# Layer 1 of a four-layer network: the product with bt ahead of the step-size means, and the gate's product in four parts

## The chip, the cores and the metric

The kernel runs on one core of a Trainium2 chip. One launch computes all four layers. The metric is the device time of that launch in microseconds (us). Six runs of the kernel before the change took 4355.97 to 4390.86 us, with a median of 4374.4 us.

A core has five engines, each with an instruction queue of its own that is worked off in order: TensorE (PE in the profile; its weight loads are shown apart as PEld), VectorE (DVE), ScalarE (ACT), GpSimd (POOL) and SyncE (SP, which here only starts transfers). Engines wait for each other through semaphores. Matrix products read SBUF, the on-chip memory, and write PSUM, a small set of accumulation buffers that the other engines read.

## The reference

x has 2 sequences of 2048 tokens with 256 features, in float32. Each of the four layers normalizes x and adds an "attention" and an "FFN" part. Only layer 1 is touched by the change. Cut to what matters, it is:

```python
xn = _layernorm(x)
x = x + attn(xn) + ffn(xn)

# attn: a selective scan
h = _layernorm(xn, ln_gamma, ln_beta)
xs, gate = split(h @ W_in)                       # 512 channels each
xs = silu(causal_conv(xs, conv_w) + conv_b)
delta = mean(softplus(xs @ Wd + bd), axis=-1)    # one step size per token
A = -exp(A_log)                                  # 16 states
Bx = (xs @ B_mat.T) * delta                      # the product with bt
h_t = exp(delta_t * A) * h_(t-1) + Bx_t          # scan over the tokens
y = h @ C_mat + D * xs
y = y * silu(gate)                               # the gate's product
attn = xn + y @ W_out

# ffn: per token and head the best of 4096 experts, by product keys
sim = q @ keys                                   # two halves, 128 keys each
index, score = best pair of keys                 # 8 heads
hidden = gelu(xn @ W_in.T + sum_heads(relu(score) * (xn . in_a[index]) * in_b[index]))
ffn = hidden @ W_out.T + sum_heads(relu(score) * (hidden . out_a[index]) * out_b[index])
```

`softplus(z)` is computed as `relu(z) + log(1 + exp(-|z|))`, with a correction for the rounding of `1 + exp(-|z|)`. That is where the four quantities `sp`, `la`, `lb` and `lc` of the kernel come from: the mean step size is the mean of `sp + la - lb + lc` over the 512 channels.

## The kernel before

x stays in SBUF for the whole launch. Layer 1 (`layer1`) cuts the 4096 tokens into 16 blocks of 256. Three generator functions do the work of one block: `scan_block` is the attention part, `choose_block` finds the experts, and `rows_block` fetches their rows and computes the FFN part. One iteration of the loop in `layer1` weaves three of them together (`weave`): the scan of block n, the choice of block n−1 and the rows of block n−2, so that each engine's queue holds work of three blocks in turn. Within that text a scheduler then orders each engine's instructions by when their inputs will be ready, so the final order isn't the text's order word for word. Layers 0, 2 and 3 lie ahead of and behind this loop.

The scan block is a chain, stage by stage:

1. Two normalizations, each followed by transposes on PE: `xn` and `xt`, then `hn` and `hT` (helpers `norm2` and `turn2`).
2. The product with `wi` (16 matmuls of two passes each). Its first half is copied to `xr` (L665), its second goes through Silu to `sgt`, the gate (L667).
3. The convolution of `xr` to `xs`: four ACT instructions (L671) and twelve on DVE (L674); then Silu over all of xs (L678).
4. The product with `wd`. For each of four channel groups m, ACT reads the sum twice from PSUM: Abs to `la` (L690) and Relu to `sp` (L691).
5. Exp of `la` (L693, behind a table load), `lb` on DVE (L695), Ln to `lc` (L697).
6. The means, `p4`: sixteen small matmuls with the constant `inv` (L702) over sp, la, lb and lc. A copy to `s4` (L705), a matmul with `four` that sums the four 32-row strips and spreads the result over 16 rows (`pd`), and the product of xs with `bt` (`pb`, four matmuls of two passes).
7. `dl`, a copy of pd (L712); `dA`, its Exp (L714, behind a table load); `dl` times `pb` on DVE (L715); the scan itself on DVE (L717).
8. For each m a matmul with `ct` and, on DVE, `xs*D + ps` written back to xs (L724).
9. The gate's product: one POOL instruction over all of xs, 128 partitions by 1024 (L727). A second POOL instruction adds xn to x (L728).
10. The product with `wout` (eight matmuls of two passes each) and its addition to x on DVE (L733).

All matmul results of the scan block come from one pool of PSUM tiles, `psc`, with two buffers (`ps_c` in the profile). A third tile is given out once one of the two has been read for the last time. The choice uses `ps_k` and the rows `ps_h`, with three buffers each. Most SBUF tiles of the scan block exist once (xs, sgt, sp, la, lb, lc, s4).

Around the chain, the same engines do the work of the other two blocks. On PE: `ps_k` (the keys), and for the rows a product into `ps_h`, transposes and the products with `dg` (L839). On DVE: max and its index (L778, L782), for each fetched row tile `G` a custom multiply-and-sum with two inputs in SBUF (L815 over 256 features, L834 over 512), its use (L817), and the addition of the rows to x (L842). On POOL: the gathers of `G`, one indirect DMA each (L805), 32 for a block, into 10 buffers. Each gather's issue occupies POOL, and it stands in the same queue as L727 and L728.

In the profile the product with bt is `ps_c<-xs,bt`, with wd `ps_c<-xs,l_wd`, with wout `ps_c<-l_wc,xs`, the means `ps_c<-sp,inv` and so on; all of them are issued from the helper `mm` (L68), the means excepted.

Of the kernel before, what the change touches and what calls it, by code (L numbers as in the profile page):

```python
# [20 lines left out]
ALU = mybir.AluOpType  # L21
# [42 lines left out]
def mm(nc, out, pairs):  # L64

    n = len(pairs)
    for i, (lhsT, rhs) in enumerate(pairs):
        nc.tensor.matmul(out, lhsT, rhs, start=(i == 0), stop=(i == n - 1))  # L68
# [93 lines left out]
def fetch_experts(g, r, pool, t):  # L162

    nc = g.nc
    y = pool.tile([P, 2, D], F32, name="yg", tag="yg", bufs=2)
    for j in range(2):
        nc.gpsimd.indirect_dma_start(y[:, j, :], None, r.yd,
                                     bass.IndirectOffsetOnAxis(ap=r.pos[:, j, t : t + 1], axis=0))
        nc.vector.scalar_tensor_tensor(g.x[:, t, :], y[:, j, :], r.wt[j][:, t : t + 1], g.x[:, t, :],
                                       ALU.mult, ALU.add)  # L170
# [390 lines left out]
def layer1(g, tc, a, r):  # L561
# [5 lines left out]
    with ExitStack() as es:  # L567
# [51 lines left out]
        for n in range(NB + 2):  # L619
            streams = []  # L620
            if n < NB:
                streams.append((1, scan_block(g, L, blocks[n], blocks[n - 1] if n % (NB // B) else None)))
            if 0 <= n - 1 < NB:
                streams.append((1, choose_block(g, L, blocks[n - 1])))
            if 0 <= n - 2:
                streams.append((2, rows_block(g, a, L, blocks[n - 2])))
            weave(*streams)


def scan_block(g, L, k, prev):  # L630
    nc, wk, TB, nt, pp = g.nc, L.wk, L.TB, L.nt, g.pp

    def pcol(name, i=0):
        return pp[:, PP[name] + i : PP[name] + i + 1]

    ti = k.tok // P
    for t in range(ti + nt if k.n else 0, min(ti + 2 * nt, NT)):
        fetch_experts(g, L.r, wk, t)
    xb = g.x[:, ti : ti + nt, :]
    k.xn = xn = wk.tile([P, nt, D], F32, name="xn1", tag="xn1", bufs=3)  # L640
    norm2(g, wk, xb, xn, nt)
    k.xt = wk.tile([P, 2, TB], F32, name="xt1", tag="xt1", bufs=3)
    turn2(g, L.psc, xn, k.xt, nt)
    yield

    hn = wk.tile([P, nt, D], F32, name="hn", tag="hn")
    norm2(g, wk, xn, hn, nt)
    hT = wk.tile([P, 2, TB], F32, name="hT", tag="hT")
    turn2(g, L.psc, hn, hT, nt, pp[:, PP["gamma"] : PP["gamma"] + 2], pp[:, PP["beta"] : PP["beta"] + 2])
    yield  # L650
    k.xr = xr = wk.tile([P, 4, TB + 3], F32, name="xr", tag="xr", bufs=2)
    if prev is None:
        nc.gpsimd.memset(xr[:, :, 0:3], 0.0)
    else:
        nc.gpsimd.tensor_copy(xr[:, :, 0:3], prev.xr[:, :, TB : TB + 3])
    sgt = wk.tile([P, 4, TB], F32, name="sgt", tag="sgt")
    for m2 in range(4):
        ps = L.psc()
        for i in range(2):
            m = 2 * m2 + i  # L660
            mm(nc, ps[:, i * TB : (i + 1) * TB],
               [(L.wi[:, c, m * P : (m + 1) * P], hT[:, c, :]) for c in range(2)])
        ps2 = ps.rearrange("p (i n) -> p i n", i=2)
        if m2 < 2:
            nc.scalar.copy(xr[:, 2 * m2 : 2 * m2 + 2, 3:], ps2)  # L665
        else:
            nc.scalar.activation(sgt[:, 2 * m2 - 4 : 2 * m2 - 2, :], ps2, AF.Silu)  # L667
    yield
    xs = wk.tile([P, 4, TB], F32, name="xs", tag="xs")
    for m in range(4):  # L670
        nc.scalar.activation(xs[:, m, :], xr[:, m, 0:TB], AF.Identity, bias=pcol("conv_b", m),  # L671
                             scale=pcol("conv_w", 4 * m))
        for c in range(1, 4):
            nc.vector.scalar_tensor_tensor(xs[:, m, :], xr[:, m, c : c + TB], pcol("conv_w", 4 * m + c),  # L674
                                           xs[:, m, :], ALU.mult, ALU.add)
        if m == 1:
            yield
    nc.scalar.activation(xs, xs, AF.Silu)  # L678
    yield


    sp = wk.tile([P, 4, TB], F32, name="sp", tag="sp")
    la = wk.tile([P, 4, TB], F32, name="la1", tag="la1")
    for m2 in range(2):
        ps = L.psc()
        for i in range(2):
            m = 2 * m2 + i
            z = ps[:, i * TB : (i + 1) * TB]
            mm(nc, z, [(L.wd[:, c, m * P : (m + 1) * P], xs[:, c, :]) for c in range(4)])
            nc.scalar.activation(la[:, m, :], z, AF.Abs, bias=pcol("bd", m))  # L690
            nc.scalar.activation(sp[:, m, :], z, AF.Relu, bias=pcol("bd", m))  # L691
    yield
    nc.scalar.activation(la, la, AF.Exp, scale=-1.0)  # L693
    lb = wk.tile([P, 4, TB], F32, name="lb", tag="lb")
    nc.vector.tensor_scalar(lb, la, 1.0, 1.0, ALU.add, ALU.subtract)  # L695
    lc = wk.tile([P, 4, TB], F32, name="lc", tag="lc")
    nc.scalar.activation(lc, la, AF.Ln, bias=g.one)  # L697

    p4 = L.psc()
    for q, (t, w) in enumerate(((sp, 0), (la, 0), (lb, 1), (lc, 0))):  # L700
        for m in range(4):
            nc.tensor.matmul(p4[32 * m : 32 * m + 32, 0:TB], L.inv[:, w, :], t[:, m, :],  # L702
                             start=(q == 0), stop=(q == 3))
    s4 = wk.tile([P, TB], F32, name="s4", tag="s4")
    nc.scalar.copy(s4, p4[:, 0:TB])  # L705
    pd = L.psc()
    mm(nc, pd[0:16, 0:TB], [(L.four, s4)])
    pb = L.psc()
    mm(nc, pb[0:16, 0:TB], [(L.bt[:, m, :], xs[:, m, :]) for m in range(4)])
    yield  # L710
    dl = wk.tile([16, TB], F32, name="dl", tag="dl")
    nc.scalar.copy(dl, pd[0:16, 0:TB])  # L712
    dA = wk.tile([16, TB], F32, name="dA", tag="dA")
    nc.scalar.activation(dA, pd[0:16, 0:TB], AF.Exp, scale=L.na)  # L714
    nc.vector.tensor_tensor(dl, dl, pb[0:16, 0:TB], ALU.mult)  # L715
    k.hs = hs = wk.tile([16, TB], F32, name="hs", tag="hs", bufs=2)
    nc.vector.tensor_tensor_scan(hs, dA, dl, 0.0 if prev is None else prev.hs[:, TB - 1 : TB],  # L717
                                 ALU.mult, ALU.add)
    for m2 in range(2):
        ps = L.psc()  # L720
        for i in range(2):
            m = 2 * m2 + i
            mm(nc, ps[:, i * TB : (i + 1) * TB], [(L.ct[:, m * P : (m + 1) * P], hs)])
            nc.vector.scalar_tensor_tensor(xs[:, m, :], xs[:, m, :], pcol("D", m),  # L724
                                           ps[:, i * TB : (i + 1) * TB], ALU.mult, ALU.add)
    yield
    nc.gpsimd.tensor_tensor(xs, xs, sgt, ALU.mult)  # L727
    nc.gpsimd.tensor_tensor(xb, xb, xn, ALU.add)  # L728
    ps = L.psc()
    for i in range(nt):  # L730
        mm(nc, ps[:, i * D : (i + 1) * D], [(xs[:, m, i * P : (i + 1) * P], L.wout[:, m, :]) for m in range(4)])
    xf = xb.rearrange("p i d -> p (i d)")
    nc.vector.tensor_tensor(xf, xf, ps, ALU.add)  # L733
    yield


def norm2(g, pool, src, dst, nt):

    nc = g.nc
    st = pool.tile([P, nt, 6], F32, name="ln_st", tag="ln_st")  # L740
    mv = pool.tile([P, nt, 2], F32, name="ln_mv", tag="ln_mv")
    for i in range(nt):
        nc.vector.bn_stats(st[:, i, :], src[:, i, :])
        nc.vector.bn_aggr(mv[:, i, :], st[:, i, :])
    rs = pool.tile([P, nt], F32, name="ln_rs", tag="ln_rs")
    nc.scalar.activation(rs, mv[:, :, 1], AF.Sqrt, bias=g.eps)
    nc.vector.reciprocal(rs, rs)
    mr = pool.tile([P, nt], F32, name="ln_mr", tag="ln_mr")
    nc.vector.scalar_tensor_tensor(mr, mv[:, :, 0], -1.0, rs, ALU.mult, ALU.mult)
    for i in range(nt):  # L750
        nc.scalar.activation(dst[:, i, :], src[:, i, :], AF.Identity, bias=mr[:, i : i + 1],
                             scale=rs[:, i : i + 1])


def turn2(g, psum, src, dst, nt, scale=None, bias=None):

    nc = g.nc
    for c in range(2):
        ps = psum()
        for i in range(nt):  # L760
            nc.tensor.transpose(ps[:, i * P : (i + 1) * P], src[:, i, c * P : (c + 1) * P], g.ident)
        if scale is not None:
            nc.scalar.activation(dst[:, c, :], ps[:, : nt * P], AF.Identity, bias=bias[:, c : c + 1],
                                 scale=scale[:, c : c + 1])
        else:
            nc.scalar.copy(dst[:, c, :], ps[:, : nt * P])
# [942 lines left out]
```

## Time and profile before

| what | value |
|---|---|
| median of six runs | 4374.4 us (4355.97 to 4390.86) |
| profiled execution | 4369.64 us |
| its span | 4367.9 us |
| granted TensorE clock, mean | 0.937 |
| L727 (gate's product), 16 times | 2346 to 2457 ns, from 1265.2 to 2257.5 us |
| L728 (x plus xn), 16 times | 1262 to 1292 ns |
| L715 (dl times pb), 16 times | 390 to 409 ns |
| L724 (xs times D plus ps), 64 times | 449 to 483 ns |
| L805 (a gather's issue on POOL), 432 times in 1300 to 2240 us | 1050 to 1071 ns in the mean |
| PE idle ahead of `ps_c<-xs,l_wd`, 1300 to 2240 us | 25.0 us |
| PE idle ahead of `ps_c<-sp,inv`, 1300 to 2240 us | 25.7 us |
| PE idle ahead of `ps_c<-l_wc,xs`, 1300 to 2240 us | 9.9 us |

How to read the profile: it shows one execution. A group's line gives the line of the kernel, the engine, the operation, what is written and read (`out<-in`), the shapes and the count; then, behind a bar, the busy time and the mean duration of one in ns; then, behind a second bar, how long the engine had been idle just ahead of these instructions, and whose end released it (`<-PE ps_c L68 8.8` means that 8.8 us of the idle time ended with a PE instruction on ps_c from line 68). "issue" is idle time that ended with nothing that the profile names. In a timeline each line has the start, the duration, the engine, the line and the operation, and in brackets the idle time before it. PE's matmuls are pipelined, and their ends are modelled.

Layer 1's loop fills about 1200 to 2300 us of the span.

### The profile page before, as it was taken

What the parts mean: (1) busy time and instruction counts of PE and PEld (TensorE: products, weight loads), DVE (VectorE), ACT (ScalarE), POOL (GpSimd) and SP (SyncE); (2) the same over time, 40 slices, a digit from 0 to 9 for tenths busy, and PEclk for the clock granted to TensorE, in tenths of its full rate; (3) what the DMA queues carried; (4) which work ended last, traced back from release to release, by engine and by line L of the source; (5) the groups of instructions that cost most, each with busy time, mean ns of one, the idle gap of its engine ahead of it and who ended that gap; (6) DMA issues with size and microseconds to landing.
All of it is one profiled execution on the core that took longest, in us unless ns stands there. A gap on an engine that the chain in (4) does not pass through costs nothing.

```text
span 4367.9 us, 58911 instructions
## 1 busy us (share of the span) xinstructions
PE 3900.2 (89%) x21516; PEld 2323.7 (53%) x21516; DVE 2509.2 (57%) x6436; ACT 1976.8 (45%) x3819; POOL 1304.5 (30%) x1306
## 2 busy tenths in 40 slices
PE   6488988999878898889885999999999999999998
PEld 5366666766645555555553777777433333333332
DVE  6354444454468888788796332333866656566560
ACT  3144333443344554445532323232555565566556
POOL 1402222222166655555464111112201111111201
PEclk7677999999999999999997999999999999999999
DMA  4200122222335666565575000000000000000000
GB/s 177 92 32 32 63 79 79 79 79 79 129 117 173 185 194 183 176 201 186 166 217 168 1 1 1 1 1 22 8 7 9 6 4 19 14 6 9 4 2 25
DMA packets 110803, 330.23 MB, mean 76 GB/s; under 512 B 30609, under 2 KB 63010, under 8 KB 104114
## 3 DMA queue, kind: packets, MB, share of 16 engines
q0 software_dynamic: 52720, 264.15, 19.5%
q1 hardware_dynamic: 55330, 59.41, 4.2%
q8 instruction: 170, 2.79, 0.3%
q10 hardware_dynamic: 2464, 2.91, 0.2%
q14 instruction: 119, 0.97, 0.1%
HBM read 286.56 MB, written 33.03 MB: 73 GB/s over the span
## 4 chain that ended last, share of the span: by engine, by line
PE 45%; DVE 4%; issue 2%; POOL 1%; ACT 1%; DMA 1%; another core or an unknown queue 0%; SPq 0%; POOLq 0%; ACTq 0%; DVEq 0%
PE ps_e L1345 12%; PE ps_v L1408 6%; PE ps_a L68 6%; PE ps_f L68 5%; PE ps_m L68 4%; PE ps_m L1350 2%; PE ps_o L1043 1%; PE ps_c L68 1%; PE ps_m L1359 1%; PE ps_k L68 1%; PE ps_s L1345 1%; DVE mp L1376 1%; PE ps_s L1350 1%; PE ps_x L68 0%; POOL G L805 0%
## 5 line engine op out<-in xcount | busy, mean ns | idle before, releaser
L1376 DVE TENSOR_REDUCE mp<-ps_m 128x1 f32<-128x512 f32 (+3 forms) x1120 | 628.4, 606 | 436.2 <-PE ps_e L1345 253.2
L1365 ACT ACTIVATE pt<-ps_e 128x512 f32<-128x512 f32 (+3 forms) x1120 | 537.2, 531 | 426.9 <-PE ps_e L1345 395.4
L1345 PE MATMUL ps_e<-qT,kT 32*128 32x512 f32 (+3 forms) x2240 | 632.2, 581 | 9.0 <-ACT pt L1365 8.8
L1350 PE MATMUL ps_m<-kT,qT 32*128 32x512 f32 (+3 forms) x2240 | 564.3, 579 | 1.1 <-DVE mp L1376 1.1
L1345 PEld LDWEIGHTS ps_e<-qT,kT 32*128 32x128 f32 x2240 | 212.3, 185 | 328.8 <-issue 122.9
L805 POOL DMA_INDIRECT G<-in_tab_in,ind x256 | 271.6, 1061 | 293.4 <-DVE ind L792 121.7
L1408 PE MATMUL ps_v<-pt,vals 128*32 128x512 f32 (+3 forms) x2560 | 307.1, 544 | 1.6 <-POOL pt L1369 0.9
L1369 POOL TENSOR_SCALAR_AFFINE_SELECT pt<-pt 128x256 f32<-128x256 f32 x256 | 104.2, 408 | 664.7 <-ACT pt L1365 664.5
L805 POOL DMA_INDIRECT G<-in_tab_out,ind x256 | 270.8, 1058 | 86.7 <-issue 58.3
L68 PE MATMUL ps_e<-xgT,we 128*128 128x256 f32 x936 | 239.7, 402 | 27.0 <-ACT xgT L306 17.7
L68 PE MATMUL ps_k<-wk,xt 128*128 128x512 f32 x512 | 261.3, 622 | 2.7 <-issue 1.4
L68 PE MATMUL ps_f<-hb,l_b 128*128 128x512 f32 x1024 | 253.2, 399 | 1.5 <-DVE hb L1034 1.5
L1033 ACT ACTIVATE hb<-ps_f 128x512 fp32r<-128x512 f32 x128 | 75.4, 596 | 321.7 <-PE ps_f L68 321.7
L68 PEld LDWEIGHTS ps_f<-hb,l_b 128*128 128x128 f32 x1024 | 190.0, 189 | 47.0 <-issue 6.7
L68 PEld LDWEIGHTS ps_e<-xgT,we 128*128 128x128 f32 x936 | 176.3, 197 | 70.2 <-ACT xgT L306 23.3
L834 DVE CUSTOM_DVE_ANT_0 scr<-hid,G,gate 128x512 f32<-128x512 f32 x256 | 198.4, 775 | 22.6 <-ACT hid L821 8.3
L1034 DVE SCALAR_TENSOR_TENSOR hb<-ps_f,hb 128x512 fp32r<-128x512 f32 x128 | 86.8, 684 | 203.7 <-ACT hb L1033 203.4
L1350 PEld LDWEIGHTS ps_m<-kT,qT 32*128 32x128 f32 x2240 | 182.3, 185 | 26.2 <-issue 22.2
L494 DVE COPY_PREDICATED AT<-lm,ps_g 128x256 f32<-128x256 uint8 x224 | 105.0, 520 | 149.5 <-PE ps_g L489 144.7
L489 PE MATMUL ps_g<-qt,E 64*128 64x64 f32 x1792 | 143.7, 303 | 32.8 <-DVE E L485 23.9
L815 DVE CUSTOM_DVE_ANT_0 scr<-xn,G,gate 128x256 f32<-128x256 f32 x256 | 144.2, 563 | 42.0 <-DMA G<-in_tab_in,ind 35.2
L817 DVE SCALAR_TENSOR_TENSOR hid<-G,lin,hid 128x512 f32<-128x512 f32 x224 | 167.1, 746 | 2.0
(421 smaller groups left out, 7665.2 us busy)
## 6 DMA issues: line engine op xcount, KB each, us to landing
xgd<-zero SPq DMA_DIRECT2D x13, 768.0 KB, 12.0
xg<-xgd SPq DMA_DIRECT2D x39, 256.0 KB, 2.9
yd<-ye SPq DMA_DIRECT2D x39, 256.0 KB, 3.3
G<-in_tab_in,ind POOLq DMA_INDIRECT x256
G<-in_tab_out,ind POOLq DMA_INDIRECT x256
kT<-qk SPq DMA_DIRECT2D x256, 16.0 KB, 1.8
out<-x SPq DMA_DIRECT2D x8, 512.0 KB, 3.0
x<-in_x ACTq DMA_DIRECT2D x4, 512.0 KB, 9.2
```

What stands on the lines that cost most here:

```text
L68: nc.tensor.matmul(out, lhsT, rhs, start=(i == 0), stop=(i == n - 1))
L489: nc.tensor.matmul(two[r][:, n * 64 : (n + 1) * 64], E[r * 64 : (r + 1) * 64, n * P : (n + 1) * P], qt[r * 64 : (r + 1) * 64, n * 64 : (n ...
L494: nc.vector.copy_predicated(AT[:, r].rearrange("p e (n t m) -> p e n t m", t=2, m=m)[:, :, :, 1, :], lm[:, li * 64 : (li + 1) * 64].unsque ...
L805: nc.gpsimd.indirect_dma_start(G, None, a[tab], bass.IndirectOffsetOnAxis(ap=k.ind[:, h, j : j + 1], axis=0))
L815: nc.vector.tensor_tensor_reduce(scr[:, 0:D], k.xn[:, j, :], G[:, 0:D], k.gate[:, h, j : j + 1], 0.0, ALU.mult, ALU.add, lin[:, h : h + 1])
L817: nc.vector.scalar_tensor_tensor(hs, G[:, D:768], lin[:, h : h + 1], hid if h == 0 else hs, ALU.mult, ALU.add)
L834: nc.vector.tensor_tensor_reduce(scr, hs, G[:, 0:512], k.gate[:, h, j : j + 1], 0.0, ALU.mult, ALU.add, lout[:, h : h + 1])
L1345: nc.tensor.matmul(te[i // step][:, i % step, c0:512], ge.kT[row(j), kt * P : (kt + 1) * P], ge.qT[row(j), qb * 512 + c0 : (qb + 1) * 512] ...
L1350: nc.tensor.matmul(tm[i // step][:, i % step, 0:w], gm.qT[row(j), qi * P : (qi + 1) * P], gm.kT[row(j), ch * 512 : ch * 512 + w], start=Tr ...
L1365: nc.scalar.activation(pt[:, o : o + step, c0:512], te[i // step][:, :, c0:512], AF.Exp, scale=0.25)
L1376: nc.vector.tensor_reduce(gm.mp[:, qi, j : j + step, ch], tm[i // step][:, :, 0:w], AX.X, ALU.max, negate=True)
L1408: nc.tensor.matmul(av[row(j), c0:512], vals[:, kt, at + 17 * j : at + 17 * j + 32], pts[j][:, c0:512], start=first, stop=last)
```

## The change

Two edits in `scan_block`. The first moves the allocation of `pb` and its four matmuls from behind the matmul with `four` to a place ahead of the means: behind Ln (L697) in the program's text. The second takes the POOL instruction over all of xs apart into four, one for each m, each placed in the loop right behind the addition L724 of the same m.

```diff
     lc = wk.tile([P, 4, TB], F32, name="lc", tag="lc")
     nc.scalar.activation(lc, la, AF.Ln, bias=g.one)
 
+    pb = L.psc()
+    mm(nc, pb[0:16, 0:TB], [(L.bt[:, m, :], xs[:, m, :]) for m in range(4)])
+
     p4 = L.psc()
     for q, (t, w) in enumerate(((sp, 0), (la, 0), (lb, 1), (lc, 0))):
         for m in range(4):
...
     nc.scalar.copy(s4, p4[:, 0:TB])
     pd = L.psc()
     mm(nc, pd[0:16, 0:TB], [(L.four, s4)])
-    pb = L.psc()
-    mm(nc, pb[0:16, 0:TB], [(L.bt[:, m, :], xs[:, m, :]) for m in range(4)])
     yield
...
             nc.vector.scalar_tensor_tensor(xs[:, m, :], xs[:, m, :], pcol("D", m),
                                            ps[:, i * TB : (i + 1) * TB], ALU.mult, ALU.add)
+            nc.gpsimd.tensor_tensor(xs[:, m, :], xs[:, m, :], sgt[:, m, :], ALU.mult)
     yield
-    nc.gpsimd.tensor_tensor(xs, xs, sgt, ALU.mult)
     nc.gpsimd.tensor_tensor(xb, xb, xn, ALU.add)
```

Line numbers in the text are those of the kernel before. In the changed kernel the four parts of the gate's product are again on line 727, the addition on 725 and x plus xn on 729; the means are on 705, s4 on 708, dl on 713, dA on 715, dl times pb on 716 and the scan on 718.

## The prediction

> **What bounds the kernel now.** I read the page's busy shares first, then the busy time of the engines in four stretches of layer 1 (the only part that the edit touches), then PE's groups of layer 1 with the idle time ahead of them, then the two edited lines, and last the order of time in one block.
>
> ```profile
> PE 3900.2 (89%) x21516; PEld 2323.7 (53%) x21516; DVE 2509.2 (57%) x6436; ACT 1976.8 (45%) x3819; POOL 1304.5 (30%) x1306
> ```
> ```profile
> 1300.00:1360.00 60.00, 48.82 (x204) 30.94 (x202) 48.64 (x152) 27.85 (x50) 35.94 (x34) 0.97 0.51 148
> 1600.00:1660.00 60.00, 54.95 (x223) 33.45 (x223) 55.90 (x187) 31.81 (x56) 38.55 (x35) 1.00 0.73 211
> 1900.00:1960.00 60.00, 51.69 (x213) 33.73 (x212) 53.41 (x176) 30.83 (x55) 35.11 (x33) 0.97 0.61 177
> 2180.00:2240.00 60.00, 52.65 (x206) 33.86 (x205) 52.03 (x164) 27.62 (x53) 36.88 (x34) 0.97 0.68 210
> ```
> The columns are the stretch, its length, busy us of PE, PEld, DVE, ACT and POOL, the granted clock, the DMA share and GB/s. Over the whole span PE looks like the bound; here neither PE nor DVE is full, though both are near 52 of 60 us. A block of 256 tokens takes 66.15 us (the gate's product L727 starts 16 times, from 1265.2 to 2257.5: 992.3/15). At 52/60 PE works some 57 us of that and idles 8 or 9. So the period is set by a serial chain (the scan block, one PSUM tile after another), filled with the work of two other blocks, and whatever shortens the chain can win at most those 9 us.
>
> ```profile
> L68 PE MATMUL ps_c<-xs,l_wd 128*128 128x256 f32 x448 | 116.3, 413 | 25.0 <-issue 19.8 <-ACT xs L678 3.6 <-ACT sp L691 1.4
> L68 PE MATMUL ps_c<-l_wc,xs 128*128 128x256 f32 x224 | 53.5, 393 | 9.9 <-POOL xs L727 9.8
> L702 PE MATMUL ps_c<-sp,inv 128*32 128x256 f32 x114 | 26.9, 438 | 25.7 <-ACT sp L691 22.6 <-issue 3.0
> L68 PE MATMUL ps_c<-xs,bt 128*16 128x256 f32 x112 | 26.5, 379 | 0.0
> ```
> These are 14 blocks (1300 to 2240 us); the last field is PE's idle time. PE waits 25.7 us ahead of the step-size means (1.8 a block), for the Relu L691, and 9.8 us for L727 (0.7 a block). The product with bt never waits: all it needs, xs, has been there since before wd.
>
> ```profile
> L727 POOL TENSOR_TENSOR xs<-xs,sgt x16: 2346/2356/2457, 1265.2 to 2257.5; 128x1024 f32<-128x1024 f32 x16
> L728 POOL TENSOR_TENSOR x<-x,xn x16: 1262/1274/1292, 1222.2 to 2184.8; 128x512 f32<-128x512 f32 x16
>   PE ps_c L68: 8.8, 9
> ```
> The third line is DVE's idle time ahead of L715 (dl times pb): 8.8 us in 9 of 16 blocks, all for bt. Now one block in order of time:
>
> ```profile
> 1838.67 0.37 ACT L705 COPY s<-ps_c 128x256 f32<-128x256 f32 x1 [1.43 <-PE ps_c L702]
> 1840.24 0.36 ACT L712 COPY dl<-ps_c 16x256 f32<-16x256 f32 x1
> 1840.62 1.28 ACT L714 ACT_TABLE_LOAD   x1
> 1841.91 0.46 ACT L714 ACTIVATE dA<-ps_c,na 16x256 f32<-16x256 f32 x1
> 1842.04 0.41 DVE L715 TENSOR_TENSOR dl<-dl,ps_c 16x256 f32<-16x256 f32 x1 [0.94 <-PE ps_c L68]
> 1843.05 1.74 DVE L717 TENSOR_TENSOR_SCAN hs<-dA,hs,dl 16x256 f32<-16x256 f32 x1
> 1842.95 1.29 POOL L728 TENSOR_TENSOR x<-x,xn 128x512 f32<-128x512 f32 x1 [2.58 <-ACT xn L751]
> 1850.49 2.37 POOL L727 TENSOR_TENSOR xs<-xs,sgt 128x1024 f32<-128x1024 f32 x1
> 1853.17 3.62 PE L68 MATMUL ps_c<-l_wc,xs 128*128 128x256 f32 x16
> 1858.66 0.68 DVE L733 TENSOR_TENSOR x<-x,ps_c 128x512 f32<-128x512 f32 x1
> ```
> From the end of L705 (1839.05) to the end of the scan (1844.78) are 5.73 us, and from the first L724 (1845.91) to wout 7.26, to L733 12.75. Between the last L724 (ends 1848.99) and L727 stands a gather that POOL had begun.
>
> **The change, part by part.** *bt.* Its 8 passes (1.89 us here, 1840.04 to 1841.93) leave the stretch between L705 and L715. Without them the stretch is: 0.55 from L705 to the matmul with `four`, 0.64 to L712, 0.36, the table load 1.28, 0.46, a hand-over of 0.1 and the scan at its usual 0.74: 4.1 us, so 1.6 less. The lower bound is what L715 shows as wait, 8.8/16 = 0.55. In this block the scan is stretched from 0.74 to 1.74 beside L728; half a microsecond earlier it would start first. But L834 (0.73) sits in DVE's queue between L715 and the scan. I take −1.3. Where bt goes it needs 1.89 us of PE: in the new order one pass pair takes the place of the first `sp` matmul, whose PSUM buffer waits for the same Relu, and three stand behind the last wd matmuls, ahead of `sp`. The 1.8 us of idle a block hide it; without that cover it costs the 1.89. Queued behind bt are the last four wd matmuls, as they were behind `sp`: no new wait. I book 0.
>
> *The gate's product.* From the two POOL rows, (2356−1274)/512 = 2.11 ns an element and 194 ns an instruction; a part of 256 is an estimated 0.73 us, four 2.94: +0.58 of POOL work a block. The parts don't wait for the fourth L724. In the new order the first three stand among the block's first gathers (0.95 us and 0.30 to issue), and the last behind at most one more. If POOL has room, the last part ends 3.08 (last L724) + 1.25 + 0.73 = 5.1 us after the first L724, 1.9 before the 6.95 of now. If POOL is full, as in this block, where gathers and L728 run almost without a gap from 1842.95 to 1850.48, the last part ends 0.58 later than now, and the 1.3 won by bt are waited for there as well: +1.9. PE may do 3/8 of wout ahead of the last part, 1.4 of 3.72 us. Against it, the order puts more filling work behind wout instead of ahead of it; half of what wout hides, 0.8, I give back. Bounds: −1.9−1.4+0.8 = −2.5 and +1.9−1.4+0.8+0.9 = +2.2, with 0.9 for a lock explained next. I take −0.7, between the ends, and on the side of a gain because wout's early part is won at either end.
>
> The lock shows in the trace: beside L727 the DVE operations with two SBUF inputs wait until it ends (L815 takes up to 3222 ns against 480 alone), 26.5 us over the 16 blocks, while L727 itself is never stretched (2346 to 2457). Four parts hold DVE for no longer in all, but DVE can slip an L834 (0.73) in between; one such slip is the 0.9 above with its hand-over.
> The Trainium skill ("SBUF — State Buffer", section "Who interferes with whom") states that such a pair is held for a whole instruction, and that the one who issues first decides; by it each of four parts may meet a DVE operation that came first, which speaks against splitting. By the row, which never shows L727 stretched, the sum stays as it is; by the rule in full, four DVE operations of 0.75 a block, it would be 48 higher, 4392.
>
> *What is moved besides.* Between wi and wd the new order has three more ps_k matmul pairs (0.86 each from start to start) and one dg product (0.43) less: +2.15 us of PE in a stretch that the convolution covers (wi starts at 1860.75, wd at 1879.47). 0 to +2.15; I take +0.4. If the cover is gone, 2.15. The table loads, the number of PE passes and the DMAs are the same in count but for one table load (1.28 us in all), and no queue of SP moves. Of POOL's gathers, the third to fifth of a block now stand behind parts that wait for L724, so L815, which already waits 26.5 us for gathers in these blocks, may wait longer; that is the rival below.
>
> *Sum.* −1.3 − 0.7 + 0.4 = −1.6 us a block, times 16: −25.6. Against the profiled execution, 4369.64 (a span of 4367.9 and 1.74 around it): 4344. The median of the six runs, 4374.4, lies 4.8 above that execution, which counts in the chances.
>
> **The rivals.** *The wait moves (no change).* The chain gets shorter, but wd still waits 19.8 us for nothing that the profile names, and PE needs its 57 of 66 us a block. For it: ACT sits idle over 6 us ahead of a block's first Abs L690 with PE's matmuls recorded as done, so PE is really later than its records, and fuller. Against it: 0.7 us a block for L727 is a wait for just this. With a fifth of the gain left, −0.3 times 16: 4365.
>
> *Parts that wait (slower).* One mechanism: a gate part at the head of POOL's queue waits for its L724 or for a DVE operation that holds the port, and gathers wait behind it, so that the last part and the gathered rows both come later. Price: each of four parts loses a DVE operation of 0.75, +3.0, and +0.58 for the instructions; with −1.3 for bt, −1.4 for wout's early part, +0.8 and +0.4 for the moved filling: +2.1 a block, +33, 4403. It decides once the last part ends 1.5 us (1.3+1.4−0.8−0.4) later against the chain than L727 does now. For it: L834 and L815 fill DVE just there, 53 of 60 us. Against it: L727's even 2.35.
>
> *More than booked (faster).* The full −1.6 of bt, −2.0 at the gate and +0.4: −3.2 a block, −51, 4318. It needs POOL to be free when the L724s end; but in the eight blocks that I followed L727 starts 1.2 to 2.5 us after the last L724, which is against.
>
> That the order would leave bt behind the means can be excluded from the instruction order for the steady blocks; it has no chance of its own.
>
> **How the numbers follow.** Forecast 0.42, no change 0.25, slower 0.23, more 0.10. A measurement of this kernel can tell some 0.5%, 22 us, from no change, so faster means under 4352 and slower over 4396, counted from the median. Faster: 0.10 and 0.38 of the forecast's 0.42: 0.48. Same: 0.04 and 0.24 of the no-change case: 0.28. Slower: 0.23 and 0.01 of the no-change case: 0.24. Range: the bounds of the terms are −1.6−2.5+0 = −4.1 a block (4304) and −0.55+2.2+2.15 = +3.8 (4430); I cut it to 4308 and 4404, which reaches through the slower rival's own price and leaves out both extremes. The forecast's own range is 4325 to 4358.
>
> **What would show it.** Right: L715 no longer waits for PE; the scan ends about 4.2 us after L705; the 25.7 us ahead of `sp` shrink by what bt takes; wout starts 4.5 to 6 us after the first L724 and L733 about 11; L727 appears 64 times at about 0.73 us; the block period is near 64.5. Wrong: gate parts of well over 0.73 us or starting long after their L724 (the lock, or the queue); more idle time of DVE ahead of L815 for gathers; the time won at the scan turning up ahead of wd or of Abs L690; or layers 0, 2 and 3, whose order is untouched, moving by more than a few microseconds.

## The result and the profile after

The changed kernel takes 4398.97 us (median of 35 runs, 4381.23 to 4417.15) against 4378.09 us of the kernel before (77 runs, 4355.67 to 4396.28): a ratio of 1.0044, 95% interval 1.0034 to 1.0053. It is slower by about 20 us. Its profiled execution has a span of 4402.8 us; the one before had 4367.9.

The busy shares and the four stretches of layer 1, in the columns of the prediction's:

```profile
PE 3911.0 (89%) x21516; PEld 2327.5 (53%) x21516; DVE 2505.7 (57%) x6436; ACT 1979.8 (45%) x3820; POOL 1326.6 (30%) x1354
```
```profile
1300.00:1360.00 60.00, 50.59 (x221) 30.71 (x220) 39.97 (x122) 33.65 (x57) 35.53 (x37) 0.97 0.49 152
1600.00:1660.00 60.00, 50.97 (x203) 30.04 (x202) 50.34 (x168) 32.76 (x55) 34.91 (x34) 0.94 0.62 188
1900.00:1960.00 60.00, 51.22 (x205) 31.27 (x204) 46.66 (x161) 31.52 (x54) 35.18 (x32) 0.94 0.59 176
2180.00:2240.00 60.00, 50.49 (x195) 31.19 (x194) 43.30 (x141) 29.95 (x50) 32.91 (x29) 0.89 0.56 166
```
The work is the same, but less of it fits into the same time: DVE is busy 180 of these 240 us instead of 210, PE 203 instead of 208. Four short stretches exaggerate: from 1300 to 2200 us DVE is busy 721 of 900 us instead of 744, PE 776 instead of 790. Something new leaves DVE idle. PE's groups of the layer's scan chain (1300 to 2240 us, 14 blocks, last field the idle time ahead):

```profile
L68 PE MATMUL ps_c<-xs,l_wd 128*128 128x256 f32 x424 | 113.2, 420 | 10.8 <-ACT sp L691 4.9 <-ACT xs L678 3.5 <-issue 2.1
L68 PE MATMUL ps_c<-l_wc,xs 128*128 128x256 f32 x224 | 67.8, 449 | 20.7 <-POOL xs L727 20.6
L68 PE MATMUL ps_c<-xs,bt 128*16 128x256 f32 x112 | 33.2, 424 | 34.5 <-issue 17.3 <-ACT sp L691 17.2
L705 PE MATMUL ps_c<-sp,inv 128*32 128x256 f32 x112 | 13.6, 454 | 13.2 <-ACT sp L691 9.9 <-issue 3.3
```
PE, which was never idle ahead of bt, now idles 34.5 us there: bt stands where `sp` stood, and 17.2 us of the wait end with the same Relu (the rest with nothing that the profile names). Ahead of wout PE idles 20.7 us, for gate parts, instead of 9.9 for the one product. And DVE's groups of the two edited stages, first before, then after:

```profile
L733 DVE TENSOR_TENSOR x<-x,ps_c 128x512 f32<-128x512 f32 x14 | 9.5, 679 | 1.9 <-PE ps_c L68 1.9
L715 DVE TENSOR_TENSOR dl<-dl,ps_c 16x256 f32<-16x256 f32 x14 | 5.7, 404 | 8.2 <-PE ps_c L68 8.1
```
```profile
L734 DVE TENSOR_TENSOR x<-x,ps_c 128x512 f32<-128x512 f32 x14 | 9.6, 686 | 20.2 <-PE ps_c L68 16.5 <-PE ps_c L762 3.7
L716 DVE TENSOR_TENSOR dl<-dl,ps_c 16x256 f32<-16x256 f32 x14 | 5.7, 407 | 3.1 <-ACT dl L713 3.0
```
DVE's wait for bt is gone, as meant: 8.1 us. In its place DVE stands idle 20.2 us ahead of the addition of wout (line 734, formerly 733). In the new order this addition stands early in DVE's queue and waits there for wout, with the other blocks' rows queued behind it. One block in order of time:

```profile
1855.69 0.37 ACT L708 COPY s<-ps_c 128x256 f32<-128x256 f32 x1 [1.43 <-PE ps_c L705]
1857.63 1.28 ACT L715 ACT_TABLE_LOAD   x1
1858.93 0.47 ACT L715 ACTIVATE dA<-ps_c,na 16x256 f32<-16x256 f32 x1
1859.43 0.74 DVE L718 TENSOR_TENSOR_SCAN hs<-dA,hs,dl 16x256 f32<-16x256 f32 x1 [0.70 <-ACT dA L715]
1862.25 0.72 POOL L727 TENSOR_TENSOR xs<-xs,sgt 128x256 f32<-128x256 f32 x1 [0.61 <-DVE xs L725]
1863.12 1.25 POOL L806 DMA_INDIRECT G<-in_tab_in,ind  x1
1864.39 1.89 POOL L727 TENSOR_TENSOR xs<-xs,sgt 128x256 f32<-128x256 f32 x2
1866.44 0.98 POOL L806 DMA_INDIRECT G<-in_tab_in,ind  x1 [0.16 <-issue]
1867.44 0.95 POOL L727 TENSOR_TENSOR xs<-xs,sgt 128x256 f32<-128x256 f32 x1
1870.90 0.69 DVE L734 TENSOR_TENSOR x<-x,ps_c 128x512 f32<-128x512 f32 x1 [1.35 <-PE ps_c L68]
```
From s4 (1856.06) to the scan's end (1860.17) are 4.1 us, the predicted value. The scan is now released by dA, behind its table load. From the first addition (1861.59) to the end of the last part are 6.8 us, hardly less than the 6.95 of before, and L734 comes 9.3 us after it instead of 12.75. So this block is faster by almost 5 us from s4 to L734's end (15.5 against 20.3). The time is lost elsewhere. The chain taken apart, as means of twelve blocks (the 4th to the 15th) of the two profiled executions, in us:

```
                                        before   after
wi's first matmul to wd's first          20.19   23.82
wd's first to the last Relu              16.07   16.54
last Relu to s4's end                     9.48    8.20
s4's end to the scan's end                5.69    4.64
scan's end to the first addition          1.47    1.65
first addition to the last gate part      6.32    7.14
first addition to L733's end             12.67   11.11
L733's end to the next block's wi         1.92    4.15
block period                             67.49   70.11
```
The edited stages (scan, gate, wout) gain 2.4 us, the step-size stage 1.3. The convolution loses 3.6, and the way from L733 to the next wi 2.2, where nothing was edited. These two executions lie 35 us apart and the medians 21, so the table shows the stages that change, and their sum (+2.62 a block) is larger than the change's own.

### The profile page after: what moved, and what is told of

Read it like the earlier page. It is cut to its first block, busy times and chain, and to the rows that moved or that the text cites. A ratio compares the mean times of both kernels' runs of the same rounds, so it can differ in the third digit from the quotient of the medians.

```text
span 4402.8 us, 58983 instructions
## 1 busy us (share of the span) xinstructions
PE 3911.0 (89%) x21516; PEld 2327.5 (53%) x21516; DVE 2505.7 (57%) x6436; ACT 1979.8 (45%) x3820; POOL 1326.6 (30%) x1354
## 4 chain that ended last, share of the span: by engine, by line
PE 69%; DVE 11%; issue 6%; ACT 5%; POOL 4%; DMA 3%; another core or an unknown queue 2%; SPq 0%; ACTq 0%; POOLq 0%; DVEq 0%
PE ps_e L1346 12%; PE ps_v L1409 6%; PE ps_g L68 6%; PE ps_e L68 6%; PE ps_a L68 6%; PE ps_f L68 5%; PE ps_m L68 4%; PE ps_c L68 4%; PE ps_k L68 2%; PE ps_g L489 2%; PE ps_m L1351 2%; PE ps_o L1044 1%; PE ps_h L840 1%; DVE scr L835 1%
## 5 line engine op out<-in xcount | busy, mean ns | idle before, releaser
L806 POOL DMA_INDIRECT G<-in_tab_out,ind x256 | 280.9, 1097 | 116.6 <-issue 56.1
L839 ACT ACTIVATE dg<-cst,lout 128x128 f32<-128x128 f32 x256 | 98.3, 397 | 168.9 <-DVE lout L835 86.2
```

The lines of the kernel that those rows point to most:

```text
L806: nc.gpsimd.indirect_dma_start(G, None, a[tab], bass.IndirectOffsetOnAxis(ap=k.ind[:, h, j : j + 1], axis=0))
```

## The experiments

All of these kernels compute the same as the kernel before. They ran on four other chips, one for each group of runs (e1 to e4; p1 and p2 with the kernels before and after; p3 to p6; q1 to q3). On each of these the kernel before has a median of 4259 to 4261 us, not 4378 (the last section tells where that differs). Each ratio is against the kernel before on the same chip. The stretches of the kernel before come from one execution on the chip of p1 and p2, so those of the other groups are compared with it across chips. The changed kernel is slower by nearly the same ratio there.

**The parts alone, each in the order that the scheduler then makes.** e1 moves only bt, e2 splits only the gate's product; their diffs are the two halves of the change.

> Only the product with bt is moved; the gate's product stays one instruction. Theory O (the loss is the order of the filling work: in the changed kernel 10.7 us of other blocks' DVE operations stand among the twelve convolution operations of a block, against 6.6 before, and PE work stands between L733 and the hn transposes): here the DVE order among the convolution is again another one, with 7 to 12 other operations, so the scan stretch falls by about 1.4 us a block and the convolution stretch grows by 2 to 4; total 4370 to 4410. Theory G (the four POOL parts cost the time by themselves, bt is a gain): 4378 minus 16 x 1.0 to 1.4, about 4356 to 4362.

> Only the gate's product is split; bt stays behind the matmul with four. Theory O: the convolution stretch grows here too (its DVE order has 8 or 9 other operations in the steady blocks), the stretch from the first addition to L733 shrinks by some 1.7 us; total 4375 to 4405. Theory G: all of the loss and more, since bt's gain is missing: 4399 plus about 20, 4410 to 4425.

e1: 1.0018 (1.0009 to 1.0027). e2: 1.0067 (1.0053 to 1.0080). bt by itself is no gain, which speaks against theory G. e2's 0.67 per cent lies between the figures of the two theories (up to 0.6, from 0.7) and doesn't choose. With e1, s4 to the scan's end takes 4.62 us, and from the end of wi to the last convolution operation pass 10.5 us. In the kernel before it was 7.0: the order changed here too.

**The convolution first.** In e3 (the changed kernel) and e4 (the kernel before) the scheduler prefers the convolution:

```diff
     for m in range(4):
-        nc.scalar.activation(xs[:, m, :], xr[:, m, 0:TB], AF.Identity, ...
+        with g.tc.high_priority(offset=120):
+            nc.scalar.activation(xs[:, m, :], xr[:, m, 0:TB], AF.Identity, ...
...
```

> The changed kernel, with the convolution's ACT and DVE instructions put ahead of other ready work by the scheduler, so that all twelve DVE operations of a block stand together. Theory O: the stretch from the end of wi to the last convolution operation falls from 10.7 us to under 4, the period by 4 to 7 us unless the other blocks' work moves into another part of the chain; at least the 21 us that the change lost come back: 4300 to 4378. Theory G: the loss stays against the kernel before with the same convolution order (next run) and the time is at most some 10 us under 4399. Theory T (DVE and PE are nearly full and only throughput counts): no difference, 4390 to 4405.

> The kernel before with the same preference for the convolution. Theory O: it gains less than the changed kernel does, since only 6.6 us of other work stand in its convolution: 4330 to 4380, and the run above, with the change on top, is faster than this one by 10 to 40 us. Theory G: this one is faster than the run above by about 20. Theory T: 4370 to 4385.

e3: 1.0038 (1.0024 to 1.0052). e4: 1.0033 (1.0021 to 1.0045). Theory O in this form falls: in both, the twelve operations of a block now stand together (5.0 and 5.1 us from first to last, against 13.7 in the changed kernel on the chip of p1), wi to wd takes 12.4 us instead of 18.4 (before) and 21.9 (changed), and nothing is won, because wd to the last Relu takes 18 instead of 10 to 11. The other blocks' work stands there now: apart from wd's own passes PE is busy 17.4 us in that stretch of e4, against 6.5 in the kernel before. Shortening a stage of the chain does not shorten the period by itself. The change no longer makes a difference between these two (1.0038 against 1.0033), so theory G, which had e4 faster by 20 us, falls too. Theory T's figure, taken against 4378 us, holds for e3 (1.0027 to 1.0062); e4 lies above it (1.0016 at most).

**The order held.** To part the edits from the order, the next kernels write out the order by hand. Each instruction of layer 1's loop on PE, DVE, ACT and POOL gets an edge to the one that stood ahead of it in a given kernel, as a fixed list; the edge demands an order and no completion.

```diff
+def hold(tc, ins):
+    for engine, text in ORDER.items():
+        mine = [i for i in ins if str(i.engine) == "EngineType." + engine]
+        rank = np.frombuffer(zlib.decompress(base64.b64decode(text)), np.uint16)
+        for a, b in zip(rank, rank[1:]):
+            tc.add_manual_dep(mine[b], mine[a].name, mybir.DependencyInfo(
+                mybir.DependencyClass.NoSync, mybir.DependencyReason.DATA), reason="order")
...
             weave(*streams)
+        hold(tc, nc.cur_bb.bb.instructions[at:])
```
p1 is both edits in the order of the kernel before, p2 the old work in the order of the changed kernel. In p1 and p3, pb's text stands behind the means' matmuls, since in the old order the first of these comes ahead of wd's end. So bt stands behind `sp` there; in the changed kernel it stands ahead of it. No run holds a kernel in its own unchanged order. That the hold by itself costs little is seen in p6 below: its ratio is 1.0008, and its wi to wd takes 18.52 us against 18.44.

> The kernel before, once more with a profile, on the same chip as the three runs beside it, so that stretches can be compared on one chip. Theories agree: the same time as the runs of before beside it.

> The changed kernel as it is, on the same chip as its companions. All theories: some 0.3 to 0.9 per cent above the kernel before on this chip.

> Both edits, with every other instruction of layer 1 held in the order of the kernel before on PE, DVE, ACT and POOL; bt stands behind the last sp matmul, the first three gate parts one gather earlier than the single product stood. Theory O (the loss is the new order of the filling work): the edits alone are a gain, 0.6 to 1.4 us a block at the scan and up to 1.4 at wout, so 0.3 to 0.9 per cent faster than before. Theory G (the gate's parts cost it by themselves): slower than before by 0.3 per cent or more, as the changed kernel is. Theory T (the three engines' total work and the port decide, order and chain hardly matter): within 0.2 per cent of before.

> Neither edit, with all other instructions of layer 1 held in the order that they have in the changed kernel; bt stands right behind the matmul with four, the single gate product where the last part stood. Theory O: slower than before by at least as much as the changed kernel, 0.5 to 1.3 per cent. Theory G: within 0.2 per cent of before. Theory T: within 0.2 per cent of before.

The kernel before took 4253.32 us in its one run here, beside a median of 4259.37. The changed kernel: 1.0039 (1.0025 to 1.0052). p1: 1.0055 (1.0041 to 1.0068). p2: 1.0086 (1.0072 to 1.0100). Means of twelve blocks, one execution of each, all on one chip, in us:

```
                             before     p2    changed    p1
work / order                old/old  old/new  new/new  new/old
wi to wd                      18.44    21.39    21.88    18.69
wd to the last Relu           10.94    10.10    10.40    10.92
last Relu to s4                8.85     7.83     7.88     9.91
s4 to the scan's end           5.59     5.62     4.52     4.85
first addition to L733        12.68    12.09    11.12    14.12
L733 to the next wi            1.97     3.91     4.05     1.98
DVE's wait for gathers         1.94     0.32     1.79     3.55
block period                  59.95    62.57    61.60    61.91
```
(The row on gathers is DVE's idle time ahead of L815 and L834 that ends with a gather's landing.) Read in steps: the new order alone costs 2.62 us a block (first to second column), at the convolution (+2.95) and behind L733 (+1.94). On top of it the edits win 0.97 (second to third): 1.10 at the scan and 0.97 at L733, less 1.1 in small losses at the other stages. Together +1.65, 26 us over 16 blocks, where the medians show 18. By the medians of the times the steps are +2.4 and −1.2 a block. But in the old order the edits, with bt behind `sp`, lose 1.96 (first to fourth; 1.5 by the medians), and the step from there to the changed kernel is −0.31. So what the order costs and what the edits are worth depend on each other. Theory O is right for p2 and wrong for p1; theory G the reverse; theory T fails for both. None holds alone. DVE's idle time ahead of wout's addition, in the kernel before and in p2 (line 742 there), both from 1300 to 2140 us:

```profile
L733 DVE TENSOR_TENSOR x<-x,ps_c 128x512 f32<-128x512 f32 x14 | 9.5, 681 | 0.2 <-PE ps_c L68 0.2
```
```profile
L742 DVE TENSOR_TENSOR x<-x,ps_c 128x512 f32<-128x512 f32 x14 | 9.6, 688 | 34.9 <-PE ps_c L75 24.5 <-PE ps_c L787 10.4
```
The wait is there without the edits, longer than in the changed kernel on that chip (19.8 us): it belongs to the order.

**Why the edits lose in the old order.** p3 holds the old order with bt alone, p4 with the four parts alone, the first three one gather ahead of the old place, p5 with all four in the old place, and p6 with two halves there:

```diff
-    nc.gpsimd.tensor_tensor(xs, xs, sgt, ALU.mult)
...
+        nc.gpsimd.tensor_tensor(xs[:, 2 * m2 : 2 * m2 + 2, :], xs[:, 2 * m2 : 2 * m2 + 2, :],
+                                sgt[:, 2 * m2 : 2 * m2 + 2, :], ALU.mult)
```

> Only bt is moved, behind the last sp matmul; every other instruction of layer 1 is held in the order of the kernel before. Theory H (bt was hidden where it stood, beside dl and dA's table load, and is not hidden in the new place, where PE has other work at all times): s4 to scan end falls by 0.7 to 1.1 us a block, Relu to s4 grows by about 1.0, the time is within 0.2 per cent of before. The forecast's own step (1.3 a block won, nothing paid): 0.4 to 0.5 per cent faster.

> Only the gate's product is split, the first three parts one gather ahead of the single product's place, the fourth in it; the rest is held in the order of before. Theory Q (a part at the head of POOL's queue waits for its addition, and a gather waits behind it): the last part ends 1 us or more later, DVE waits longer for gathers (2.1 us a block before), 0.3 to 0.6 per cent slower. Theory L (the port: four holds in place of one): slower by as much, and the next run too. The forecast's step: 0.7 us a block, 0.25 per cent faster.

> Only the gate's product is split, all four parts in the place of the single one, so that no gather is moved behind a part; the rest is held in the order of before. Theory Q: the last part ends 0.6 us later, wout starts its first products up to 2 us earlier, L733 comes 0 to 0.8 us earlier, and the time is from 0.3 per cent faster to the same. Theory L: 0.3 to 0.6 per cent slower, as the run above.

> The gate's product in two halves, each 128x512, both in the place of the single one, the rest held in the order of before. Theory Q: the second half ends 0.2 us later than the single product, half of wout's first products run ahead of it; from 0.3 per cent faster to the same. Theory L: between before and the run above, 0.1 to 0.3 per cent slower.

p3: 1.0030 (1.0020 to 1.0041). p4: 1.0041 (1.0028 to 1.0054). p5: 1.0026 (1.0016 to 1.0036). p6: 1.0008 (0.9999 to 1.0017), no difference that is clear.

```
                            before      p3      p4      p5      p6
last Relu to s4               8.85   10.01    8.83    8.85    8.85
s4 to the scan's end          5.59    4.79    5.55    5.54    5.57
first addition to last part   6.37    6.75    6.94    7.03    6.34
first addition to wout        6.93    7.63    5.78    6.21    6.44
wout's end to L733            1.39    1.36    2.77    2.54    1.86
DVE's wait for gathers        1.94    2.15    3.43    2.96    1.89
first addition to L733       12.68   13.33   13.36   13.45   12.77
block period                 59.95   60.94   61.08   60.66   60.15
```
bt (p3) wins 0.80 at the scan and pays 1.16 ahead of s4, so theory H holds in its mechanism, and the time is worse than its 0.2 per cent: 0.65 more goes between the first addition and L733. The parts (p4, p5) do let wout start up to 1.15 us earlier, and its products end earlier, and yet L733 comes later. One block of the kernel before (on the chip of p1 and p2), DVE and POOL, and the like block of p5 (where the held order's code shifts the line numbers):

```profile
1913.53 2.35 POOL L727 TENSOR_TENSOR xs<-xs,sgt 128x1024 f32<-128x1024 f32 x1
1916.04 0.99 POOL L805 DMA_INDIRECT G<-in_tab_in,ind  x1 [0.16 <-issue]
...
1920.56 0.48 DVE L815 CUSTOM_DVE_ANT_0 scr<-xn,G,gate 128x256 f32<-128x256 f32 x1 [0.67 <-DMA G<-in_tab_in,ind]
1920.97 0.75 DVE L817 SCALAR_TENSOR_TENSOR hid<-G,lin,hid 128x512 f32<-128x512 f32 x1
1921.64 0.68 DVE L733 TENSOR_TENSOR x<-x,ps_c 128x512 f32<-128x512 f32 x1
```
```profile
1928.32 2.76 POOL L735 TENSOR_TENSOR xs<-xs,sgt 128x256 f32<-128x256 f32 x4
1931.24 0.99 POOL L831 DMA_INDIRECT G<-in_tab_in,ind  x1 [0.16 <-PE ps_h L75]
...
1935.80 0.48 DVE L841 CUSTOM_DVE_ANT_0 scr<-xn,G,gate 128x256 f32<-128x256 f32 x1 [0.70 <-DMA G<-in_tab_in,ind]
1936.20 0.75 DVE L843 SCALAR_TENSOR_TENSOR hid<-G,lin,hid 128x512 f32<-128x512 f32 x1
1936.87 0.68 DVE L742 TENSOR_TENSOR x<-x,ps_c 128x512 f32<-128x512 f32 x1
```
In both, L733 starts 5.8 us behind the end of the gate's product (1915.88 and 1931.08), because DVE works off an L815 ahead of it that waits for the first gather which POOL issues behind the gate (it lands at 1920.54 and 1935.77). DVE waits for that gather in 7 of the twelve blocks of the kernel before and in 11 of p5; in the others it is still at the rows ahead of L733. Over twelve blocks the distance from the gate's end to L733 is 5.64 us in the kernel before, 5.75 in p4, 5.74 in p5 and 5.90 in p3. Wout isn't what ends last there. The longer the gate holds POOL, the later that gather, and with it L733; DVE's whole wait for gathers grows by 1.0 us a block in p5 and 1.5 in p4. p4 against p5 shows no clear extra price of the parts ahead of a gather (the intervals overlap). Theory Q's gain for p5 isn't met. Theory L has the sign right, at the lower edge of its figures (0.26 per cent, where it says 0.3 to 0.6); the stretches tie the loss to POOL's queue, but no run parts that from the port.

**L733 out of that queue.** The last three move L733 in DVE's held order ahead of the last L815 and L817: q1 with the old gate, q2 with four parts in place, q3 with two.

> The kernel before in its own order, with one thing moved: on DVE the addition L733 stands two row operations earlier (ahead of an L815 that waits for a gather issued behind the gate's product, and of an L817). Theory J (L733 ends last not by wout but by that gather, 5.8 us behind the gate's end): the gap between wout's end and L733 falls from 1.4 to under 0.5, the next block's chain starts a microsecond earlier; 0.2 to 0.5 per cent faster. Theory T (what L733 gains, DVE or PE lose elsewhere): within 0.15 per cent.

> The gate's product in four parts in the place of the single one, as measured before at 0.26 per cent slower, now with L733 two row operations earlier. Theory J: wout's earlier end (0.4 us) now counts, L733 is no longer bound to the gate's end plus 5.8 us, and the time is 0.3 per cent or more below that run: 0.3 faster to 0.0. Theory T, or POOL's 0.6 us a block as the price by itself: stays 0.15 to 0.3 per cent slower.

> The gate's product in two halves in the place of the single one (0.08 per cent slower before), with L733 two row operations earlier. Theory J: the fastest of all, 0.3 to 0.6 per cent faster than the kernel before. Theory T: within 0.15 per cent.

q1: 1.0011 (1.0000 to 1.0022). q2: 1.0023 (1.0013 to 1.0033). q3: 1.0014 (1.0004 to 1.0024).

```
                          before      q1      p5      q2      q3
wout's end to L733          1.39    0.40    2.54    0.46    0.43
first addition to L733     12.68   11.67   13.45   10.88   11.05
L733 to the next wi         1.97    2.98    2.02    3.26    3.13
wi to wd                   18.44   18.81   18.41   19.13   18.99
```
Theory J holds for the stage and falls for the time. L733 comes 1.0 us earlier in q1, and the next wi starts as much later after it. In q2 it comes 2.6 earlier than in p5; 1.24 of that is lost ahead of wi and 0.72 ahead of wd. The 0.6 us left in that one execution the times don't show: q2's interval overlaps p5's. No kernel of the study is faster than the one before. Theory T describes all three. q2's 0.23 per cent is the size of POOL's extra 0.6 us a block (9.6 us in all), but that this is its cause is not shown.

## Why the prediction was wrong

The step that failed is the term for what is moved besides, +0.4 us a block: the new order of the other work alone costs 2.6. It loses from wi to wd (+2.95), which the prediction called covered, and from L733 to the next wi (+1.94), for which it has no term. The two edits, in that order, win about half of the 2.0 forecast for them. The paragraphs below take the terms in the prediction's order.

*What bounds.* "Whatever shortens the chain can win at most those 9 us" was the wrong start. It took PE's idle time for slack that a shorter chain turns into time. In the kernel before, on the chip of p1 and p2, a period of 59.95 us holds 57.3 us of PE and 55.9 of DVE, and in four cases a shorter stage gave no shorter time: the convolution in e3 and e4, L733 in q1 and q2. Only beside the new order did shorter stages win time (0.97 a block, second to third column above). In-order queues filled with two other blocks' work pass a gain on as a wait at the next stage (q1: L733 1.0 us earlier, the next wi 1.0 later behind it). The rival "the wait moves" named this and was given 0.25.

*bt, −1.3.* At the scan the mechanism was right and the size a little high: 4.1 us in the block shown; as a mean −0.80 (old order) or −1.10 (new). For the new place "I book 0" nearly holds: with the order the same (p2 against the changed kernel), wd to s4 grows by 0.35 us, though PE has far less idle time ahead of `sp` on that chip than the 1.8 us a block that were to hide it (from 1300 to 2140 us: 0.0 in the kernel before, 4.8 in p2). The prediction's "without that cover it costs the 1.89" is closer to the old order, where bt stands behind `sp`, between it and the other means: there it costs 1.16 (p3), more than the 0.80 won. Where it stood before it ran beside dl and dA's table load (1.28 us), which the scan waits for in any case.

*The gate, −0.7.* The sizes hold in part: +0.58 of POOL work (p5's last part ends 0.66 later), wout starts earlier. In the new order, for which the term was meant, L733 comes 0.97 earlier (p2 against the changed kernel, both edits), near the forecast; there L733 starts 0.15 us behind wout. In the old order it comes 0.68 to 0.77 later, because the step from wout to L733 does not hold there: I took L733 to end with wout, though the gap of 1.9 us between wout's end and L733 stood in the timeline I showed. That the new order had already moved L733 was luck for this term. Between the last L724 and L727 in the block that I showed stand the rest of one gather and a whole second one (1849.54 to 1850.48), not one. The lock is there in both kernels: DVE's operations beside the gate's product are longer than their medians by 26.6 us over the 16 blocks before and by 19.0 after, and the parts themselves by 7.8.

*What is moved besides, +0.4.* This is the term that failed: 2.62 us a block (p2; 2.4 by the medians) against bounds of 0 to 2.15. I counted PE's filling between wi and wd, 2.15 us, and called it covered by the convolution. The cover failed, for the convolution itself ends later: from the end of wi to its last DVE operation pass 7.0 us in the kernel before and 10.7 in p2. DVE's queue had been reordered there as well: in the trace of before 6.3 us of other blocks' operations stand among the twelve of the convolution, in that of after 10.0. And L733 moved ahead in DVE's queue, where DVE now waits 20.2 us from 1300 to 2240; the way from L733 to the next wi (+1.94) has no term in the sum. The prediction speaks of DVE's order nowhere but around the gate.

*The sum.* −1.6 was forecast: −2.0 for the two edits and +0.4 for the order. The executions of the changed kernel and of the one before on one chip have +1.65 (+1.1 by the medians): −0.97 for the edits in their order and +2.62 for the order. From the first gate product to the last, as the prediction took its 66.15 us a block, it is 67.94 in the changed kernel, where 64.5 was forecast. The measured 4399 lies within the range given and near the price of the slower rival (4403), but that is luck. The rival's mechanism is there: parts have a median of 818 ns against the 730 estimated, eight waits of POOL for an addition add up to 15.1 us, and with the order held the parts lengthen DVE's wait for gathers by 1.0 to 1.5 us a block. But it was to decide once the last part ends 1.5 us later, and that is 0.8 (7.14 against 6.32); and with the order the same the two edits together are a gain. As the cause of the 20 us it was not confirmed.

*Left open.* Which item of the new order costs most: the orders of the four engines were only held together. The stages that grow are shown; that DVE's order rather than PE's makes them grow is argued. Why the edits lose in the old order is shown for the stages, not for the time: moving L733 out of the way (q1, q2) gave none of it back. And the granted clock falls with the time. Over the twelve blocks it is 0.981 in the kernel before, 0.968 in the changed one and 0.966 in p2, and PE is busy 57.3, 58.3 and 58.2 us a block. A slower PE can so be up to 1.0 of the +1.65 or 0.9 of the +2.62; whether it is a cause or comes from PE's new gaps was not tried. It is not the whole: e1 and e4, on another chip, have periods of 60.7 and 61.0 us at 0.988 and 0.986.

## What to carry to other kernels

Where a scheduler orders several streams into in-order queues, an edit has two effects, its own and that of the new order. Price the second on every engine, stage by stage, also where nothing was edited, and part the two by holding the order. Before moving work off a chain, ask what else the next operation waits for (here a table load, and a row operation two places ahead in the same queue that waits for a gather), and whether the engines have room at all.

## What the runs showed that was not expected

The same kernel in the same order took 4368 us of span on one chip and 4252 on another (that of p1 and p2), and nearly all of it lies in layer 1: a block period of 67.5 us against 60.0. DVE's wait ahead of the maxima, in the same window of 840 us (1300 to 2140), first in the profile before the change, then on the other chip:

```profile
L778 DVE TENSOR_REDUCE mx<-ps_k 128x4 f32<-128x512 f32 x96 | 65.6, 683 | 61.7 <-remote 39.5 <-PE ps_k L68 22.2
```
```profile
L778 DVE TENSOR_REDUCE mx<-ps_k 128x4 f32<-128x512 f32 x110 | 75.4, 685 | 7.1 <-PE ps_k L68 6.7
```
"remote" is a release that the profile ties to no recorded instruction; what L778 reads is PE's result in ps_k. So on the first chip results of PE seem to reach DVE late, by more than PE's recorded matmuls explain; the granted clock is 0.95 there and 0.98 here over layer 1 (1300 to 2200 and 1300 to 2140 us). What makes PE late was not tried. The ratio of the change is the same on both, 1.0044 and 1.0039.
